# A convolution-attention model in one kernel: pieces of side work kept off the first two turns of a segment, and their ScalarE operations issued a turn later

## The chip, the cores and the metric

The kernel runs on one core of one Trainium2 chip. The metric is the time of the launch on the device, in microseconds, as the median of three runs. One further execution was taken with the hardware profiler; all durations below come from it.

## The reference, cut to what matters

The input is an image batch of four, 64 x 64 pixels with 128 channels, in fp32. Two layers follow each other.

```python
# layer 0, for each of the 4 images, N = 4096 pixels
c1 = conv3x3(elu(x), W1) + b1                    # 128 -> 128
a, b = split(conv3x3(c1, W2) + b2)               # 128 -> 2 x 128
c3 = a * sigmoid(b)
q, k, v = c3 @ Wq + bq, c3 @ Wk + bk, c3 @ Wv + bv   # 4, 4, 16 wide
atten = softmax(q @ k.T / 4, strictly causal) @ v
x = x + c3 + tile(atten, 8) @ W3 + b3
# layer 1, t = x as 4096 tokens
y = layernorm(t)
h = y + attention(y, 16 heads of 8, full) @ wo
t = t + h + (silu(h @ w1) * (h @ w3)) @ w2
y2 = layernorm(t)
t = t + mixture_of_8_experts(y2, top 2)
```

By far the largest part is the full attention of layer 1: 16 heads over 4096 queries and 4096 keys, for four images. Each score has to go through an exponential.

## The kernel before

**Steps.** The attention of layer 1 is cut into steps. A step (`attention_step`, L774) takes four heads (a group g), 512 queries (a block c) and 128 keys (kt): its part `scores` issues four matmuls into two PSUM tiles `s` of 128 x 1024 (there are three such buffers) and two exponentials on ScalarE into tiles `e`; its part `values` issues the matmuls of e with the values `vg` that add up in the PSUM tile `acc`. There is one `acc`, one bank. The causal attention of layer 0 has steps of its own (`first_step`, L699), 36 for each image. In all there are 4096 + 144 = 4240 steps, hence 8480 exponentials.

**Segments.** All steps of one g and c, or a part of their keys, are a segment. `plan` (L1101) lists 152 segments in a fixed order: for image 0 first segments over a quarter of the keys (8 of 8 steps), then over half of them (16 segments of 8 or 16 steps), then over the rest (32 of 16 or 32 steps); 32 of 32 steps for each later image. `stream()` (L1118) walks over the plan and gives out one step after the other; if a segment's operands are not there yet it gives None. It issues, on SP's queue, the loads of queries (`qx`), values (`vg`) and keys (`f_kx` from `d_k`) ahead of their use. After a segment's last values VectorE copies `acc` to a tile `at` (or adds it to an earlier part). Where the segment ends the keys, `by_token` is put into the list `urgent` and runs one turn after the next; otherwise `at` is stored to DRAM.

**Turns.** The main loop (L1184) runs once per turn: it issues the scores of one step, inserts at most one piece of other work, and then issues values. `finish(2)` holds the values of two steps back: in a turn, the values are those of the step of two turns ago. All engines work in the order written (`InOrder`), each instruction as soon as what it waits for is there.

**Pieces.** All other work is written as generators. A `yield us, kind` ends a piece and gives its TensorE time; `fillers` is the list of generators and works from its front. `convolutions` (L392), `first_attention` (L525) and `second_operands` (L604) prepare an image, under one filler of 149 us; `last_part` (L833, 20.8 us) finishes 512 tokens of an image. A piece that ends with "held" is the first half of one that shares the PSUM bank `m`. The turn's budget, `credit`, grows by `rate`; `rate` is 1 while image 0 is prepared and later the work left in `fillers` over the steps left to 40 before the image's end. A piece is inserted when the credit is positive, or when the stream waits, or when something urgent may run.

**Inside the pieces.** `winograd` (L341) computes a 3 x 3 convolution of 16 image rows in four column terms q with two pairs of products each; `final` makes the output of q = 2 and q = 3. For the gate half of the second convolution `final` adds on VectorE and issues a tanh on ScalarE; the rest (`gates`) is kept in the list `late` until the next pair. `elu` (in `convolutions`) treats chunks of 512 pixels in a pipeline of three stages: c_ (transposes on TensorE and evictions), b_ (the sum `pos`), a_ (the minimum `neg` and its exp). `last_part` has a tanh after each of three products and an exp of the router.

Before the main loop `run_alone` prepares the first two blocks of image 0 with no steps beside; after it the last part of the last block runs alone.

Of the kernel before, what the change touches and what calls it, by code (L numbers as in the profile page):

```python
# [115 lines left out]
def fast_path(ctx: ExitStack, tc: tile.TileContext, a: dict, where: dict, out: bass.AP, verdict):  # L116
# [33 lines left out]
    def chunk(tag, name=None):  # L150
        return wk.tile([P, QB], FP, tag=tag, bufs=CHUNKS.get(tag, 1), name=name or tag)
# [10 lines left out]
    def bank():  # L162
        return s_tile()[:, :QB] if alone[0] else m_tile()
# [177 lines left out]
    def winograd(u, cols, v, bias, used, final):  # L341

        late = []
        for q, j in enumerate(COLS):
            sd = chunk("sd")
            s, d = wk.tile([P, QB // 2], FP, tag="sums", bufs=1, name="sums"), sd[:, : QB // 2]
            for pair in ((1, 2), (0, 3)):
                ps = bank()
                part = [ps[:, : QB // 2], ps[:, QB // 2 :]]
                for m, i in zip(part, pair):  # L350
                    product(m, u[:, 4 * i + j, cols], v[q][:, i])
                    if i == pair[0]:
                        yield 0.46, "held"
                if pair[0] == 1:
                    if alone[0]:
                        act.activation(sd, ps, AF.Copy)
                    else:
                        dve.tensor_copy(sd, ps)
                    dve.tensor_tensor(s, d, sd[:, QB // 2 :], ALU.add)
                    dve.tensor_tensor(d, d, sd[:, QB // 2 :], ALU.subtract)  # L360
                    while late:
                        late.pop(0)()
                else:
                    t = chunk("neg", "t2")
                    if q == 0:

                        dve.scalar_tensor_tensor(t[:, : QB // 2], part[0], bias, s, ALU.add, ALU.add)
                        dve.scalar_tensor_tensor(t[:, QB // 2 :], d, bias, part[1], ALU.add, ALU.subtract)
                    else:
                        dve.tensor_tensor(t[:, : QB // 2], part[0], s, ALU.add)  # L370
                        dve.tensor_tensor(t[:, QB // 2 :], d, part[1], ALU.subtract)
                    used(q)
                    if q == 0:
                        one = t
                    elif q == 1:
                        both, less = chunk("pos", "both"), chunk("pos", "less")
                        (dve if alone[0] else pool).tensor_tensor(both, one, t, ALU.add)
                        pool.tensor_tensor(less, one, t, ALU.subtract)
                    elif q == 2:
                        late.append(final(0, t, both, ALU.add))  # L380
                    else:
                        late.append(final(1, less, t, ALU.subtract))
                yield 0.46, "stop"
        if late[0] is not None:
            yield 0.0, "stop"
            late.pop(0)()

# [4 lines left out]
    def convolutions(b, st):  # L392
# [4 lines left out]
        def elu(n):  # L397

            todo = range(made[0], n)
            made[0] = max(made[0], n)  # L400
            neg, pos = {}, {}
            for at in range(len(todo) + 2 if todo else 0):
                a_, b_, c_ = (todo[i] if 0 <= i < len(todo) else None for i in (at, at - 1, at - 2))
                if c_ is not None:
                    r, k = divmod(c_, 2)
                    ps = bank()
                    transposed(pos[c_], ps)
                    put = [(r, slice(1 + 8 * k, 9 + 8 * k), slice(0, 8))]
                    if k == 0 and r > 0:
                        put.append((r - 1, slice(17, 18), slice(0, 1)))  # L410
                    if k == 1 and r < 3:
                        put.append((r + 1, slice(0, 1), slice(7, 8)))
                    for band, to, of in put:
                        dve.tensor_scalar(
                            e_band[band % 2][:, to, 1 : IMG + 1], rows(ps)[:, of], -1.0, None, ALU.add
                        )
                if b_ is not None:

                    pos[b_] = chunk("pos")
                    dve.scalar_tensor_tensor(pos[b_], xs[b_], 0.0, neg[b_], ALU.max, ALU.add)  # L420
                    if b_ + 2 < NQ:
                        xs.append(load_x(b, b_ + 2, "xe"))
                if a_ is not None:
                    neg[a_] = chunk("neg")
                    dve.tensor_scalar(neg[a_], xs[a_], 0.0, None, ALU.min)
                    act.activation(neg[a_], neg[a_], AF.Exp)
                yield (0.0 if c_ is None else 0.6), "stop"

        def first(r):
            band = c_band[r % 2]  # L430
            inner = tiles(band[:, 1:17, 1 : IMG + 1])

            def final(h, x, y, op):
                x, y = (ap.rearrange("p (i y x) -> p i y x", i=2, y=8) for ap in (x, y))
                dve.tensor_tensor(inner[:, :, :, :, h], x, y, op)
                return lambda: None

            return final

        def second(r, gate):  # L440
            c3 = st.c3
            whole = tiles(c3.rearrange("p (y x) -> p y x", x=IMG))

            def final(h, x, y, op):
                shape = "p (i y x) -> p i y x"
                to = whole[:, :, :, :, h]
                if not gate:
                    x, y = (ap.rearrange(shape, i=2, y=8) for ap in (x, y))
                    dve.tensor_tensor(to, x, y, op)
                    return lambda: None  # L450

                g = x if h == 0 else y
                dve.tensor_tensor(g, x, y, op)
                act.activation(g, g, AF.Tanh, scale=0.5)
                g = g.rearrange(shape, i=2, y=8)

                def gates():
                    for i in range(2):
                        dve.scalar_tensor_tensor(to[:, i], g[:, i], 1.0, to[:, i], ALU.add, ALU.mult)

                return gates

            return final

# [368 lines left out]
    def last_part(b, c):  # L833
# [25 lines left out]
        for n, (lo, size) in enumerate(FCH):  # L859
            ps = bank()  # L860
            yield from halves(ps, fw1[:, lo : lo + size], hT, size)
            h1, th = chunk("neg", "h1"), chunk("sd", "th")
            dve.tensor_copy(h1[:size], ps[:size])
            act.activation(th[:size], h1[:size], AF.Tanh, scale=0.5)
            yield 0.46, "stop"
            ps = bank()
            yield from halves(ps, fw3[:, lo : lo + size], hT, size)
            dve.scalar_tensor_tensor(h1[:size], ps[:size], 0.5, h1[:size], ALU.mult, ALU.mult)
            dve.scalar_tensor_tensor(gT[n][:size], th[:size], 1.0, h1[:size], ALU.add, ALU.mult)
            yield 0.46, "stop"  # L870
# [52 lines left out]
        dve.tensor_reduce(m0, lg, AX.X, ALU.max)  # L923
        dve.tensor_tensor(lg, lg, over(m0), ALU.subtract)
        pr = small("pr", [4, NE])
        act.activation(pr, lg, AF.Exp)
        yield 0.95, "stop"
        yield 0.0, "stop"
        m1, w1 = top(pr, "a")
        rest = small("rest", [4, NE])  # L930
# [182 lines left out]
                        plan.append(Segment(b, run, g, c, 0, 4 * n, n, base))  # L1113
            had = n
    steps_left = [sum(s.hi - s.lo for s in plan if s.b == b) for b in range(B)]
    now = [0]

    def stream():  # L1118
        in_kx, vg_of = [None] * 4, {}
# [15 lines left out]
        for at, seg in enumerate(plan):  # L1135
# [12 lines left out]
            follower = plan[at + 1] if at + 1 < len(plan) else None  # L1148
            for kt in range(seg.lo, seg.hi):
                steps_left[seg.b] -= 1  # L1150
                if seg.lo > 0 and kt == seg.lo + 4:

                    part.append(chunk("part"))
                    sp.dma_start(out=part[0], in_=scratch[seg.b]["p"][seg.g, seg.c])
                yield attention_step(seg.b, seg, kt, 8 * seg.place(kt // 8) + kt % 8, qx, vg, part)
                if follower and follower not in ahead and follower.ready():
                    bring(follower)
                if kt % 8 == 7:

                    for later in plan[at + 1 :]:  # L1160
                        quarters = [q for q in range(later.lo // 8, later.hi // 8) if later.place(q) == seg.place(kt // 8)]
                        if quarters:
                            if later.ready():
                                key_quarter(later, quarters[0])
                            break
# [18 lines left out]
    while True:  # L1184
# [19 lines left out]
            within = steps_left[b] - 40 if b + 1 < B else min(steps_left[b] - 40, 160)  # L1204
            rate = sum(us for _, us in fillers) / max(1, within)
        credit = min(0.7, credit + rate)
        if waiting or credit > 0.0 or urgent and not held[0]:
            credit -= insert()
        finish(2)
    finish(0)  # L1210
# [724 lines left out]
```

## Time and profile before

| | |
|---|---|
| runs | 8383.02, 8379.8, 8378.74 us; median 8379.8 us |
| profiled execution | 8383.2 us; its span, first to last instruction, 8381.4 us |
| granted TensorE clock, mean | 0.981 |
| ScalarE (ACT) busy | 7919.2 us, of it 7836.1 us in 8480 exponentials |
| TensorE (PE) busy | 8082.3 us |
| VectorE (DVE) busy | 2543.8 us |
| GpSimd (POOL) busy | 711.6 us |
| TensorE waiting for the copy of acc (`at`) | 60.4 us in 53 waits |
| ScalarE waiting for scores (`s`) | 180.7 us in 164 waits |
| ScalarE waiting for VectorE's `t` (gate) and `neg` (elu) | 33.6 and 43.3 us |

In the lines of a profile a group is named by its output and inputs, as `e<-s`, with its shapes and count; after the bar stands its busy time and the mean of one in ns, and after the second bar the time that the engine stood idle just before such instructions, with what ended it. In an order of time each line has its start, its length and, in brackets, the idle time before it with its releaser. `PE m` is the bank of pieces, `PE s` the scores. Matmuls are pipelined, so a busy TensorE need not be at its peak. Most instructions carry one line number, that of the helper which issues them, so they are told apart by tile names.

### The profile page before, as it was taken

What the parts mean: (1) busy time and instruction counts of PE and PEld (TensorE: products, weight loads), DVE (VectorE), ACT (ScalarE), POOL (GpSimd) and SP (SyncE); (2) the same over time, 40 slices, a digit from 0 to 9 for tenths busy, and PEclk for the clock granted to TensorE, in tenths of its full rate; (3) what the DMA queues carried; (4) which work ended last, traced back from release to release, by engine and by line L of the source; (5) the groups of instructions that cost most, each with busy time, mean ns of one, the idle gap of its engine ahead of it and who ended that gap; (6) DMA issues with size and microseconds to landing.
All of it is one profiled execution on the core that took longest, in us unless ns stands there. A gap on an engine that the chain in (4) does not pass through costs nothing. (4 is left out here: it accounts for less than half of the span.)

```text
span 8381.4 us, 173763 instructions
## 1 busy us (share of the span) xinstructions
PE 8082.3 (96%) x73785; PEld 2565.1 (31%) x73785; DVE 2543.8 (30%) x5279; ACT 7919.2 (94%) x8698; POOL 711.6 (8%) x597
## 2 busy tenths in 40 slices
PE   4899999999999999999999999999999999999998
PEld 3222222223333332333333233233333333332333
DVE  7433122223322223333332222333333332221123
ACT  1899999999999999999999999999999999999996
POOL 5101101000000003110000000311100000000000
PEclk7999999999999999999999999999999999999998
DMA  1221010101100001101110000001101111011110
GB/s 54 76 66 66 19 38 23 40 23 48 44 17 19 22 11 31 33 29 46 34 30 11 26 15 17 28 30 44 33 33 43 37 37 43 31 38 34 54 53 32
DMA packets 239541, 295.99 MB, mean 35 GB/s; under 512 B 81731, under 2 KB 153891, under 8 KB 238755
## 3 DMA queue, kind: packets, MB, share of 16 engines
q1 hardware_dynamic: 234739, 283.03, 10.6%
q8 instruction: 580, 9.50, 0.5%
q10 hardware_dynamic: 4016, 1.77, 0.1%
q14 instruction: 206, 1.69, 0.1%
HBM read 185.12 MB, written 99.61 MB: 34 GB/s over the span
## 5 line engine op out<-in xcount | busy, mean ns | idle before, releaser
L105 ACT ACTIVATE e<-s 128x1024 f32<-128x1024 f32 x8480 | 7836.1, 1083 | 191.0 <-PE s L105 180.7
L105 PE MATMUL acc<-e,vg 128*9 128x512 f32 x32768 | 4362.5, 598 | 61.2 <-DVE at L105 60.4
L105 PE MATMUL s<-qx,f_kx 32*128 32x512 f32 (+1 forms) x16960 | 2795.9, 497 | 68.3 <-ACT e L105 51.4
L105 PEld LDWEIGHTS s<-qx,f_kx 32*128 32x128 f32 (+1 forms) x16960 | 1121.4, 182 | 4074.7 <-ACT e L105 3821.9
L105 PEld LDWEIGHTS acc<-e,vg 128*9 128x9 f32 x32768 | 707.3, 90 | 861.3 <-issue 448.5
L105 PE MATMUL m<-v,f_wino 128*32 128x256 f32 x5360 | 435.1, 397 | 9.6 <-DVE t L105 7.1
L105 DVE TENSOR_TENSOR by_e<-m,gate 128x512 f32<-128x512 f32 x248 | 171.5, 691 | 869.3 <-PE m L105 869.3
L105 POOL TENSOR_TENSOR v<-r 128x1024 f32<-128x1024 f32 x128 | 249.4, 1954 | 1277.4 <-PE m L105 1258.1
L105 DVE COPY sd<-m 128x512 f32<-128x512 f32 x167 | 115.5, 691 | 726.0 <-PE m L105 726.0
L105 PE MATMUL m<-f_we,y2T 128*32 128x256 f32 x3968 | 318.4, 393 | 0.5 <-DVE nt L105 0.5
L105 POOL TENSOR_TENSOR rs<-ve,f_minus_half 128x4 f32<-128x4 f32 x64 | 65.2, 1019 | 2972.5 <-DVE ve L105 2819.6
L105 DVE TENSOR_REDUCE added<-by_e 128x128 f32<-128x1024 f32 x128 | 255.2, 1994 | 4.4
L105 POOL TENSOR_TENSOR t<-t,h 128x512 f32<-128x512 f32 x32 | 40.9, 1278 | 2456.3 <-DVE h L105 2456.3
L105 PE MATMUL m<-hT,f_fw 128*32 128x256 f32 (+1 forms) x2728 | 236.1, 391 | 0.0
L105 DVE TENSOR_TENSOR t<-m,sums 128x256 f32<-128x256 f32 x126 | 53.5, 425 | 465.5 <-PE m L105 465.5
L105 DVE SCALAR_TENSOR_TENSOR h<-m,h 128x512 f32<-128x512 f32 (+1 forms) x93 | 64.2, 690 | 411.3 <-PE m L105 411.3
L105 DVE TENSOR_TENSOR t<-m,t 128x512 f32<-128x512 f32 x62 | 42.9, 692 | 446.3 <-PE m L105 446.3
L105 DVE COPY h<-m 128x512 f32<-128x512 f32 (+1 forms) x93 | 64.2, 690 | 357.0 <-PE m L105 357.0
L105 PEld LDWEIGHTS m<-v,f_wino 128*32 128x32 f32 x5360 | 107.1, 108 | 177.2 <-issue 152.5
L105 DVE COPY at<-acc 128x512 f32<-128x512 f32 x130 | 89.6, 689 | 233.2 <-PE acc L105 232.7
L105 PE MATMUL m<-e,f_v 128*32 128x512 f32 (+2 forms) x1128 | 149.7, 574 | 0.0
L105 DVE TENSOR_TENSOR e<-e,f_consts 128x128 f32<-128x128 f32 x128 | 30.2, 295 | 346.9 <-ACT e L105 346.9
(259 smaller groups left out, 3751.3 us busy)
## 6 DMA issues: line engine op xcount, KB each, us to landing
f_kx<-d_k SPq DMA_DIRECT2D x139, 512.0 KB, 4.1
qx<-d_q SPq DMA_DIRECT2D x152, 256.0 KB, 2.7
d_q<-two SPq DMA_DIRECT2D x64, 512.0 KB, 3.6
vg<-d_v SPq DMA_DIRECT2D x32, 576.0 KB, 4.2
d_k<-two SPq DMA_DIRECT2D x32, 512.0 KB, 3.3
d_v<-vc SPq DMA_DIRECT2D x32, 288.0 KB, 3.1
xe<-in_x_dram SPq DMA_DIRECT2D x32, 256.0 KB, 2.9
xt<-in_x_dram SPq DMA_DIRECT2D x32, 256.0 KB, 3.8
```

Of the source, the lines that this page charges most:

```text
L105: made = op(*args, **kw)
```

## The change

In the first two turns of a segment no piece is inserted unless the stream waits or something urgent may run; the first segment and those whose operands were not brought ahead are excepted (`quiet`). In `winograd` the tanh of the gate is no longer issued with its addition but at the start of the next pair, the entries of `late` are taken one at each pair's start, and what is left is given out with an empty piece each; layers without a gate leave nothing in `late`. In `elu` the stages b_ and a_ come ahead of c_. In `last_part` the tanh and the router's exp are issued at the start of the following piece.

```diff
@@ winograd
             for pair in ((1, 2), (0, 3)):
+                if late:
+                    late.pop(0)()
                 ps = bank()
...
-                    while late:
-                        late.pop(0)()
...
-                        late.append(final(0, t, both, ALU.add))
+                        late += final(0, t, both, ALU.add)
                     else:
-                        late.append(final(1, less, t, ALU.subtract))
+                        late += final(1, less, t, ALU.subtract)
                 yield 0.46, "stop"
-        if late[0] is not None:
+        while late:
             yield 0.0, "stop"
             late.pop(0)()
@@ elu
+                if b_ is not None:
+                    pos[b_] = chunk("pos")
+                    dve.scalar_tensor_tensor(pos[b_], xs[b_], 0.0, neg[b_], ALU.max, ALU.add)
+                    if b_ + 2 < NQ:
+                        xs.append(load_x(b, b_ + 2, "xe"))
+                if a_ is not None:
+                    neg[a_] = chunk("neg")
+                    dve.tensor_scalar(neg[a_], xs[a_], 0.0, None, ALU.min)
+                    act.activation(neg[a_], neg[a_], AF.Exp)
                 if c_ is not None:
...
-                if b_ is not None:
...
-                if a_ is not None:
...
@@ first(r) and second(r, gate), final
-                return lambda: None
+                return []
...
-                act.activation(g, g, AF.Tanh, scale=0.5)
-                g = g.rearrange(shape, i=2, y=8)
+                by_y = g.rearrange(shape, i=2, y=8)
+
+                def tanh():
+                    act.activation(g, g, AF.Tanh, scale=0.5)
 
                 def gates():
                     for i in range(2):
-                        dve.scalar_tensor_tensor(to[:, i], g[:, i], 1.0, to[:, i], ALU.add, ALU.mult)
-
-                return gates
+                        dve.scalar_tensor_tensor(to[:, i], by_y[:, i], 1.0, to[:, i], ALU.add, ALU.mult)
+
+                return [tanh, lambda: None, gates]
@@ last_part
             dve.tensor_copy(h1[:size], ps[:size])
+            yield 0.46, "stop"
             act.activation(th[:size], h1[:size], AF.Tanh, scale=0.5)
-            yield 0.46, "stop"
...
         pr = small("pr", [4, NE])
+        yield 0.95, "stop"
         act.activation(pr, lg, AF.Exp)
-        yield 0.95, "stop"
+        yield 0.0, "stop"
         yield 0.0, "stop"
@@ stream and the main loop
-    now = [0]
+    now, quiet = [0], [False]
...
                 steps_left[seg.b] -= 1
+
+                quiet[0] = kt < seg.lo + 2 and at > 0 and not late
...
-        if waiting or credit > 0.0 or urgent and not held[0]:
+        if waiting or credit > 0.0 and not quiet[0] or urgent and not held[0]:
             credit -= insert()
```

## The prediction

> **What bounds the kernel now.** I read the page first, then ScalarE's waits past the start-up (600 to 8315 us), then the order of time around single waits. On the page:
>
> ```profile
> PE 8082.3 (96%) x73785; PEld 2565.1 (31%) x73785; DVE 2543.8 (30%) x5279; ACT 7919.2 (94%) x8698; POOL 711.6 (8%) x597
> L105 ACT ACTIVATE e<-s 128x1024 f32<-128x1024 f32 x8480 | 7836.1, 1083 | 191.0 <-PE s L105 180.7
> ```
>
> Two engines look full, but only one is. ScalarE does 8480 exponentials in 7836.1 us, 0.924 us each, so a turn (two of them) costs 1.85 us. For TensorE I took starts of the scores from the order of time: 5000.47, 5002.34, 5003.74. A turn with a piece takes 1.87 us, a turn without one 1.40. About two turns in three hold a matmul piece after batch 0, so TensorE's mean is near 1.7 us: it runs ahead of ScalarE by the three score buffers and waits for them (its weight loads wait 3822.7 us for e). **ScalarE sets the pace; what counts is where it stands idle.** The whole idle time is 8381.4 - 7919.2 = 462 us. Its waits from 600 to 8315:
>
> ```profile
> ACT e L105 <- PE s L105: 117.4, 138, 5.2
> ACT t L105 <- DVE t L105: 20.1, 22, 1.5
> ACT neg L105 <- DVE neg L105: 7.3, 6, 2.9
> ACT e L105 <- ACT e L105: 1.9, 9, 0.3
> ```
>
> The columns are the total, the number and the longest. So 147 us lie in the long middle; the other 315 are start-up, the two changes of batch 0's key range, and the tail. Why scores come late is seen at 4340 us, the last turns of a segment's results:
>
> ```profile
> 4341.75 1.94 DVE L105 TENSOR_REDUCE added<-by_e 128x128 f32<-128x1024 f32 x1
> ...
> 4343.93 0.68 DVE L105 COPY at<-acc 128x512 f32<-128x512 f32 x1
> 4344.67 0.12 PEld L105 LDWEIGHTS acc<-e,vg 128*9 128x9 f32 x8 [2.33 <-DVE at L105]
> 4344.67 1.04 PE L105 MATMUL acc<-e,vg 128*9 128x512 f32 x8 [1.85 <-DVE at L105]
> ...
> 4346.24 4.69 ACT L105 ACTIVATE e<-s 128x1024 f32<-128x1024 f32 x5 [1.96 <-PE s L105]
> ```
>
> The copy of acc stands in VectorE's queue behind a piece's sum of 1.94 us. TensorE may not overwrite acc, waits 1.85 us, and the next scores stand behind those values: ScalarE is idle 1.96 us. The second kind is direct:
>
> ```profile
> 5903.68 1.67 DVE L105 TENSOR_TENSOR t<-t,both 128x512 f32<-128x512 f32 x1
> ...
> 5905.72 0.63 ACT L105 ACTIVATE t<-t 128x512 f32<-128x512 f32 x1 [1.49 <-DVE t L105]
> 5906.25 7.41 ACT L105 ACTIVATE e<-s 128x1024 f32<-128x1024 f32 x8
> ```
>
> The tanh waits for VectorE though two exponentials of the next turn could run; the line below shows that they start only after it.
>
> **The Trainium skill.** "TensorE: Matmul & The Clock Gate", Part 1, says that TensorE falls to half clock after an idle window of about 3.4 us and needs a busy one to return. The trace agrees: after the 4.43 us wait at 8007 the eight values take 1.90 us, not 1.04, and a second ScalarE wait of 1.45 us follows. "ScalarE: Activation LUTs", Table sets, puts exp and tanh in one set, so a moved tanh costs no table load; the trace has one load in all. "Perfetto Trace Analysis", Per-engine timelines, has each ScalarE instruction wait in a queue ahead of the engine; the 1.49 us above shows that queue blocking.
>
> **The change part by part.**
>
> (1) Quiet turns. The values of a step trail it by two turns, so the last values of a segment are issued at the end of its follower's second turn and the copy right behind them; the follower's first values come a turn later. VectorE's work ahead of the copy is that of pieces in turns 1 and 2: just the turns that become empty. In the listing of VectorE, 38 of the 133 copies past 700 us begin without idle time before them, that is, behind a piece. I went through ScalarE's 41 waits of 0.8 us or more past 700 us (83.1 us) and looked for a wait of acc for at within 6 us before each: 18 places, with their repeats at half clock 57.1 us; two more at 497 and 543 add 3.6. Of these 60.7 I take **50**. The rest may stay: a layernorm piece (at 8002 it keeps VectorE until 8006.5) issued in the turn just before the segment still reaches the copy. Bounds 35 and 61.
>
> (2) Tanh later. Direct waits 20.1 us, and 4.6 more from 260 to 435; five waits of 1.3 us follow such a tanh by 4 to 8 us (at 1146, 1528, 3665, 3859, 5733: 6.6 us). Of these 31 I take **29**: the tanh now comes after another pair of exponentials, 1.85 us, against waits of at most 1.49. The gates come two pieces later and no engine but VectorE needs them soon. Bounds 20 and 31. The 96 tanh and 32 exp of the last part, moved likewise, had no wait outside the tail, as VectorE was done early: 0. In the tail ScalarE waits for VectorE either way. Were the cover gone (VectorE a turn behind), each could wait up to 1.5 us as the tanh above; being issued a turn later makes that less likely, not more.
>
> (3) The elu order. Exp waits for two VectorE operations (0.69 and 0.42 us) and no more for the eviction behind TensorE's transposes. Of 7.3 us I take **6** (4 to 7). The load of xe keeps its place in SP's queue.
>
> (4) Lost turns. While batch 0 is prepared the credit is full and every turn takes one piece, so a quiet turn delays preparation by a turn. The first stage has 8 segments of 8 turns; 7 of them lose 2: 14 turns. That stage already ends too early (busy time of each engine in the stretch, then ScalarE's order of time):
>
> ```profile
> core 0: us, PE busy (x) PEld busy (x) DVE busy (x) ACT busy (x) POOL busy (x), PEclk, DMA share, GB/s
> 360.00:378.00 18.00, 9.60 (x114) 3.44 (x106) 10.32 (x16) 0.86 (x1) 0.00 (x0) 0.69 0.62 208
> ```
>
> ```profile
> 377.14 5.65 ACT L105 ACTIVATE e<-s 128x1024 f32<-128x1024 f32 x6 [17.83 <-PE s L105]
> ```
>
> ScalarE, busy 0.86 of 18 us, stands 17.83 us until the second key range is stored (d_k issued at 368.31) and loaded. The 14 pieces move into this bare gap. There, from 358.4 to 368.3, some six pieces took 10 us; but first-attention steps moved with them bring ScalarE's own work along. At about 1 us each I add **13** (0 to 25). The second stage: preparation ends at 718.51 (the last d_k), its last segment's eighth turn, where keys for the third range are fetched, is at 793: 39 turns of slack. It loses 15 x 2 quiet turns and some 4 for more yields, 34: free, by 5 turns. If that cover goes, a late load as above, some 10 us.
>
> From batch 1 on the rate is worked out anew each turn from what is left, pieces use about 0.8 of the turns (with empty ones), and quiet takes 64 of 1024: 0.94 are left, so 0. The extra yields (net 4 a batch, and one in each last part) are turns without matmul. A crowded turn after the quiet ones costs TensorE 1.87 against 1.85: hidden by the lead that the two empty turns of 1.40 give.
>
> DMAs: pieces moved two turns bring their stores and loads behind the follower's qx and vg in SP's queue; these are issued in turn 1 and used a segment later. In batch 0 the order of d_k and f_kx may shift single waits (one of 6.6 us stands at 488): plus or minus 7. The start-up reorders elu and tanh too, with ScalarE idle for DVE t and neg there: plus or minus 5, taken as 0, since a longer chain is at its place.
>
> **Sum**: -50 - 29 - 6 + 13 = -72 us. The profiled execution took 8383.2 us around a span of 8381.4, 3.4 above the median of 8379.8, so it is a usual one; 8383.2 - 72 = 8311 for it, and 8379.8 - 72 = **8308** for the median.
>
> **Rivals.** (A) The forecast, 0.68. (B) The wait moves on: VectorE's backlog comes from the turn before the segment or the crowded third turn, so that of the 60.7 us only 20 go, and tanh gives 20. For it: layernorms and sums of 2 to 6 us; 0.38 us waits for at with no backlog. Against: in the cases read, the late operation belonged to a matmul of turn 2. Time: 8380 - 20 - 20 - 5 + 13 = 8348. 0.20. (C) Slower: batch 0 starves. If the second stage's slack of 39 turns is less than what quiet turns and yields take, preparation ends after the stage; then both gaps are bare: 14 + 34 pieces at 2.2 us (two chained matmul halves, eviction and a wait) = 106, less 85 of gains: 8401. It decides from 39 lost turns on; I count 34. 0.06. (D) The flag hardly acts: it is skipped where a piece is urgent, and stays as it was during first-attention steps. But an urgent piece is born only at the end of turn 2, and such steps start after a turn with a piece, where the flag is off. Then only tanh and elu would count, some -35, or -15 if the pieces then crowd: 8345 to 8365. 0.06.
>
> **Numbers.** Best case: 61 + 31 + 7 and some 15 of the 35.6 us of short waits (104 under 0.8 us) gained, nothing lost: 8266. The low side of A and B is 8379.8 - 35 - 20 - 4 + 35 = 8356. Range 8266 to 8356; that leaves out C and some of D. A measurement of this kernel tells about 0.2% (17 us) from no change: faster 0.88, same 0.06, slower 0.06.
>
> **What would show it.** Right: PE's wait of acc for at falls from 60.4 to below 25; ACT's wait for t to under 3 and for neg in the middle to about 1; the idle time before e from 600 to 8315 from 117 to 60-75; the gap at 377 grows to about 30 us; busy times of ScalarE stay at 7919. Wrong: acc's wait stays over 40 (B or D), a new gap near 800 us (C), or ScalarE's idle falls while TensorE's busy share in the middle reaches 99% with the turn no shorter.

## The result and the profile after

The changed kernel takes **8297.96 us** (median of four runs, 8293.22 to 8302.43) against 8381.41 us (8378.74 to 8385.31) of the kernel before beside it: a ratio of 0.990, 95% interval 0.9883 to 0.9917. That is 83.4 us less; the forecast was 72 less. The profiled execution took 8302.43 us around a span of 8300.7 us, so it is the longest of the four.

The page of the changed kernel, its busy times and two groups (after the second bar: the idle time just before such instructions):

```profile
PE 8073.1 (97%) x73713; PEld 2576.8 (31%) x73713; DVE 2557.3 (31%) x5278; ACT 7915.4 (95%) x8699; POOL 708.5 (9%) x597
...
L105 ACT ACTIVATE e<-s 128x1024 f32<-128x1024 f32 x8480 | 7842.5, 1087 | 133.4 <-PE s L105 124.3
L105 PE MATMUL acc<-e,vg 128*9 128x512 f32 x32768 | 4337.9, 595 | 1.7 <-DVE at L105 1.7
```

ScalarE has the same work, 7915.4 us against 7919.2; its idle time fell from 462.2 to 385.3 us, and these two differences (76.9 + 3.8) are the 80.7 us between the spans. TensorE's wait for the copy of `acc` is nearly gone: 1.7 us, where the same line of the kernel before has 60.4:

```profile
L105 PE MATMUL acc<-e,vg 128*9 128x512 f32 x32768 | 4362.5, 598 | 61.2 <-DVE at L105 60.4
```

ScalarE's waits in the long middle, 600 to 8235 us (total, number, longest; the middle ends 80 us earlier than before's):

```profile
ACT e L105 <- PE s L105: 53.8, 88, 3.1
ACT neg L105 <- DVE neg L105: 7.4, 4, 3.3
ACT e L105 <- ACT e L105: 1.5, 8, 0.2
```

Scores now cost it 53.8 us instead of 117.4, the tanh (`t`) nothing instead of 20.1, the elu's exp (`neg`) 7.4 as before. From 600 us to the last exponential (which ends at 8310.84 us before, at 8223.18 after) ScalarE's whole idle time fell from 154.5 to 68.7 us, by 85.8, and waits with a name make up 84 of it. Both ends lost a little. The tail behind the last exponential took 77.5 us instead of 70.5, and by 600 us ScalarE had done 358.75 us of work, against 360.76.

The end of a segment, in order of time in the changed kernel:

```profile
4354.65 10.22 ACT L105 ACTIVATE e<-s 128x1024 f32<-128x1024 f32 x11
...
4358.01 1.05 PE L105 MATMUL acc<-e,vg 128*9 128x512 f32 x8
...
4359.12 0.69 DVE L105 COPY at<-acc 128x512 f32<-128x512 f32 x1 [9.06 <-PE acc L105]
4359.87 1.05 PE L105 MATMUL acc<-e,vg 128*9 128x512 f32 x8
```

The copy finds VectorE idle for 9.06 us, starts as soon as the last values are there, and the follower's first values come 0.06 us after it ends (4359.12 + 0.69 = 4359.81) with no wait in brackets. ScalarE's line, from 4354.65 for 10.22 us, runs through without a break. And the tanh:

```profile
5885.05 1.67 DVE L105 TENSOR_TENSOR t<-t,both 128x512 f32<-128x512 f32 x1
...
5890.96 0.68 ACT L105 ACTIVATE t<-t 128x512 f32<-128x512 f32 x1
5891.48 5.66 ACT L105 ACTIVATE e<-s 128x1024 f32<-128x1024 f32 x6
```

It runs 4.2 us after its addition ends (5890.96 - 5886.72), so its input has long been there.

What it paid: the gap before image 0's second key range, ScalarE's order of time.

```profile
387.10 5.65 ACT L105 ACTIVATE e<-s 128x1024 f32<-128x1024 f32 x6 [36.91 <-PE s L105]
```

The 17.83 us have become 36.91.

### The profile page after: what moved, and what is told of

It is laid out like the page before. It is cut to its first block, busy times and chain, and to the rows that moved or that the text cites. A ratio compares the mean times of both kernels' runs of the same rounds, so it can differ in the third digit from the quotient of the medians.

```text
span 8300.7 us, 173662 instructions
## 1 busy us (share of the span) xinstructions
PE 8073.1 (97%) x73713; PEld 2576.8 (31%) x73713; DVE 2557.3 (31%) x5278; ACT 7915.4 (95%) x8699; POOL 708.5 (9%) x597
## 4 chain that ended last, share of the span: by engine, by line
PE 87%; issue 7%; DVE 3%; ACT 1%; POOL 1%; DMA 1%; SPq 0%; ACTq 0%; POOLq 0%; DVEq 0%
PE acc L105 41%; PE s L105 28%; PE m L105 18%; ACT e L105 1%; DVE h L105 1%; DVE added L105 0%; DMA nt<-d_a 0%; DVE t L105 0%; POOL v L105 0%; DMA f_kx<-d_k 0%; POOL rs L105 0%; DVE two L105 0%; DMA xe<-in_x_dram 0%; DVE at L105 0%; DVE by_e L105 0%
```

## The experiments

Each was timed in five rounds beside the kernel before. Ratios are to that kernel, with the 95% interval. "Changed kernel" means the kernel after.

**1. Quiet turns alone**, all else as before.

```diff
-        if waiting or credit > 0.0 or urgent and not held[0]:
+        if waiting or credit > 0.0 and not quiet[0] or urgent and not held[0]:
```

> Only the quiet turns are added to the kernel before; the order of ScalarE's operations and of elu stays. Theory (the parts add up): TensorE's wait of acc for at falls from 60 to about 2 us as in the changed kernel, the gap before the second key range grows from 18 to about 37 us, ScalarE's direct waits for the gate's t stay near 20 us past 600 us: 8381 - 57 + 15 = about 8340. Rival (the two parts overlap: without the later tanh the crowded turns after the quiet ones lose again what was won): 8360 or more. Rival (quiet is all that counts): 8300.

Measured 8328.05 us, 0.9934 (0.9921 to 0.9948), -53.9 us. ScalarE's waits past 600 us:

```profile
ACT e L105 <- PE s L105: 59.5, 104, 2.8
...
ACT t L105 <- DVE t L105: 20.1, 22, 1.2
```

Past 600 us TensorE's wait for `at` fell from 54.8 to 1.1 us, and the waits for scores by 57.9 us, while the tanh waits stayed at 20.1 us to the tenth. So the quiet turns act on the first kind of wait only, and on nearly all of it. The gap was 34.78 us long.

**2. Later ScalarE operations alone**: the changed `winograd`, `final` and `last_part`, without the quiet turns and the elu order.

> Only the later ScalarE operations (the gate's tanh, the last part's tanh and exp) are added to the kernel before; elu and the inserting of pieces stay. Theory: the waits for t past 600 us go from 20 to about 0, acc's wait for at stays at 55 to 60, the gap before the second key range stays near 18: 8381 - 29 = about 8352. Rival (the tanh was covered by ScalarE's own queue, the gain was in the quiet turns): 8375 to 8385.

Measured 8318.70 us, 0.9924 (0.991 to 0.9937), -63.2 us: twice what was expected. The tanh wait was gone as expected, but waits for scores fell too, from 117.4 to 82.3 us, and TensorE's wait for `at` in the middle was down by more than a quarter, from 54.8 us:

```profile
PE acc L105 <- DVE at L105: 39.4, 36, 6.5
```

Nothing in the moved tanh explains this directly. It does bring more empty pieces with it (the entries of `late`), and these shift every later piece against the ends of segments. Run 5 tests that.

**3. The elu order alone.**

> Only the order of elu's three stages is changed in the kernel before. The prediction gave it 6 us. Theory now, from the changed kernel's order of time: the min waits for the load of xe, which waits for the sum before it; with the stages nearer together this load is less covered, so the waits for neg past 600 us stay at 6 to 10 us and the time within 5 us of 8381. Rival (the eviction ahead was the cause, the rest came from elsewhere): neg below 2 us and 8375 or less.

Measured 8388.97 us, 1.0011 (1.0004 to 1.0017), +7.1 us: a small loss. Its waits from 600 to 8235 us:

```profile
ACT e L105 <- PE s L105: 120.8, 125, 5.2
ACT t L105 <- DVE t L105: 20.2, 22, 1.5
ACT neg L105 <- DVE neg L105: 10.0, 6, 2.9
```

Again six waits of the elu's exp, with the same longest of 2.9 us; their total rose from 7.3 to 10.0. The reorder doesn't remove what that exp waits for, which is of two kinds. In the kernel before three of the six (4.8 us) are for an image's first load of `xe`. In the changed kernel, VectorE's and ScalarE's order of time at such a place:

```profile
788.40 0.43 DVE L105 TENSOR_SCALAR neg<-xe 128x512 f32<-128x512 f32 x1 [5.80 <-DMA xe<-in_x_dram]
...
788.86 0.63 ACT L105 ACTIVATE neg<-neg 128x512 f32<-128x512 f32 x1 [3.34 <-DVE neg L105]
```

The minimum waits for a load that was issued at 783.03, one piece earlier. The median load of `xe` takes 2.9 us from issue to landing, more than a turn of 1.85. At an image's first chunk there is no eviction yet that could stand ahead of the minimum.

Two more (2.1 us) are behind VectorE operations that run beside GpSimd's `v` (terms of the next convolution). The first of these places in run 3:

```profile
3168.73 8.00 POOL L105 TENSOR_TENSOR v<-r 128x1024 f32<-128x1024 f32 x4
...
3172.47 2.47 DVE L105 SCALAR_TENSOR_TENSOR pos<-xe,neg 128x512 f32<-128x512 f32 x1 [6.08 <-ACT neg L105]
...
3174.87 2.14 DVE L105 TENSOR_SCALAR neg<-xe 128x512 f32<-128x512 f32 x1
...
3175.00 1.11 PE L105 MATMUL m<-f_consts,pos 128*128 128x128 f32 x4 [1.08 <-DVE pos L105]
...
3177.04 0.63 ACT L105 ACTIVATE neg<-neg 128x512 f32<-128x512 f32 x1 [2.77 <-DVE neg L105]
```

The sum took 2.47 us and the minimum 2.14, against medians of 0.69 and 0.43; the exp waited for the minimum and TensorE's transposes for the sum. At the two places of this kind the exp waited 2.77 and 2.73 us, in the kernel before 0.99 and 1.07. Right behind them ScalarE waited for scores 4.2 us (1.80, 0.71 and 1.73), before 0.6. Together that is 7.1 us more, about as much as run 3 lost. Only one wait of the kernel before, 0.4 us, stood behind an eviction. The order alone doesn't settle whether sum and minimum meet `v`: run 11 below, in the old order, has waits of 1.07 and 2.71 us there.

**4. Quiet turns only once image 0 is prepared.**

```diff
-                quiet[0] = kt < seg.lo + 2 and at > 0 and not late
+                quiet[0] = kt < seg.lo + 2 and at > 0 and not late and batches[0].second == NQ
```

> The changed kernel with quiet turns only once image 0 is prepared. Theory (lost turns lengthen the gap before the second key range): the gap falls from 37 back to about 18 us, some waits of acc for at return before 720 us (8 waits, about 8 us, of which ScalarE feels 5): 8298 - 19 + 5 = about 8284. Rival (the longer gap is ScalarE work that only changed its place, so nothing is lost by it): 8298 or up to 8305.

Measured 8295.75 us, 0.9895 (0.988 to 0.9911): 2.2 us below the changed kernel, where 14 had been expected. The gap did shrink to 14.43 us. The core's busy times from 0 to 600 us, first the changed kernel, then this one (the fourth pair of numbers is ScalarE):

```profile
core 0: us, PE busy (x) PEld busy (x) DVE busy (x) ACT busy (x) POOL busy (x), PEclk, DMA share, GB/s
0.00:600.00 600.00, 464.15 (x3602) 185.15 (x3602) 308.77 (x589) 358.75 (x405) 165.15 (x150) 0.87 0.20 65
```

```profile
core 0: us, PE busy (x) PEld busy (x) DVE busy (x) ACT busy (x) POOL busy (x), PEclk, DMA share, GB/s
0.00:600.00 600.00, 467.02 (x3798) 188.46 (x3798) 321.47 (x615) 367.82 (x412) 168.94 (x153) 0.88 0.21 66
```

22.5 us less gap gave 9.1 us more of ScalarE's work by 600 us, since gaps of 7.03 us at 356 and 5.29 us at 488 came in; and the middle's idle time, up to the last exponential, was 73.8 us, 5.1 more, about as much as the elu's exp waited more (12.2 against 7.4 us). The two kernels' runs overlap, so the 2.2 us are no measurable gain. The length of one gap is a poor price for lost preparation: work that doesn't stand in it comes out elsewhere.

**5. The empty pieces without the later tanh**: run 2, with the tanh and the exp issued where they were before.

```diff
-                def tanh():
-                    act.activation(g, g, AF.Tanh, scale=0.5)
+                act.activation(g, g, AF.Tanh, scale=0.5)
...
-                return [tanh, lambda: None, gates]
+                return [lambda: None, lambda: None, gates]
```

> The kernel before with only the number of pieces changed as in the later-ScalarE kernel: the same empty pieces are added and dropped, and the gates come as late, but every tanh and exp is issued at its old place; no quiet turns, old elu. It shows what the shift of all pieces against the segments' ends does by itself. Theory (of the 63 us that the later-ScalarE kernel won, some 30 are tanh waits and the rest is that other pieces now fall on the segments' ends): waits for t stay near 20 us past 600 us, acc's wait for at falls from 55 to about 40, time 8381 - 63 + 30 = about 8348. Rival (all 63 us come from the later tanh, by stalls of TensorE that follow a tanh): acc's wait near 55, time 8375 to 8385.

Measured 8350.99 us, 0.9964 (0.995 to 0.9977), -31.0 us.

```profile
ACT e L105 <- PE s L105: 90.4, 121, 7.0
...
ACT t L105 <- DVE t L105: 20.0, 22, 1.2
```

So half of run 2's gain comes without any tanh moved: scores wait 27.0 us less (117.4 - 90.4), though the profiled run was the slowest of the five (8360.01 us). The later tanh itself is the rest, 8350.99 - 8318.70 = **32.3 us**. This kernel moves pieces only by what a few more empty ones take; where they then stand against the ends of 152 segments is chance. It gives out the gates later, too, as run 2 does; but of the 47 waits for `at` past 600 us in the kernel before only one, 0.9 of 54.8 us, had a gate right ahead of the copy, so that can explain little.

**6 and 7. One quiet turn each**: only the second (`kt == seg.lo + 1`), and only the first (`kt == seg.lo`), in the changed kernel.

> The changed kernel with only a segment's second turn empty; pieces go into the first again. Theory (VectorE has the whole second turn of 1.4 to 1.9 us to finish a piece of the first; only long ones, layernorms and sums of 2.9 to 6 us, still reach the copy): acc's wait for at past 600 us rises from 1 to 5 to 12 us, the gap before the second key range falls from 37 to about 28 us: 8298 plus or minus 6. Rival (the first turn's pieces matter as much): acc's wait 25 or more, 8320.

> The changed kernel with only a segment's first turn empty; pieces go into the second again. Theory (the second turn's pieces stand right ahead of the copy): acc's wait for at is near that without quiet turns, 35 to 55 us, time 8298 + 20 to 8298 + 40, less 8 us of the shorter gap: 8310 to 8330. Rival (the first turn is the one that counts): 8300 or less and acc's wait under 15 us.

Only the second: 8286.49 us, 0.9888 (0.9873 to 0.9903), 11.5 us *below* the changed kernel and below what was expected, though TensorE's wait for `at` came back in part (7.7 us); the gap was 29.78 us instead of 36.91. The runs do not overlap (8283.56 to 8289.22 against 8293.22 to 8302.43), though the intervals of the ratios overlap. Only the first: 8347.55 us, 0.9961 (0.9947 to 0.9975), slower than the 8310 to 8330 expected, and 29 us slower than run 2, which has no quiet turn at all (nor the new elu order, which alone cost 7). TensorE's wait, then the order of time at one place, both with only the first turn quiet:

```profile
PE acc L105 <- DVE at L105: 54.6, 49, 4.4
```

```profile
7442.49 1.11 DVE L105 TENSOR_SCALAR y<-t,mv,rs 128x128 f32<-128x128 f32 x4 [1.20 <-POOL rs L105]
7443.52 0.68 DVE L105 COPY at<-acc 128x512 f32<-128x512 f32 x1
...
7444.26 1.79 PE L105 MATMUL acc<-e,vg 128*9 128x512 f32 x8 [4.42 <-DVE at L105]
...
7446.88 1.94 ACT L105 ACTIVATE e<-s 128x1024 f32<-128x1024 f32 x2 [4.89 <-PE s L105]
```

A layernorm stands right ahead of the copy, with GpSimd's step (1.20 us) inside it. A piece held back in turn 1 is inserted in turn 2, straight ahead of the copy. The turn that does most of the work is the second. The first buys a little and costs more. In the profiled runs (18.9 us apart in span) ScalarE's idle time from 600 us to the last exponential was 74.9 us with the second turn alone, 6.2 more than with both. But it had done 371.08 us of work by 600 us instead of 358.75, and the tail took 71.1 us instead of 77.5. So the first turn's price lies in the preparation of image 0 and in the tail, not in the long middle.

**8. A layernorm with one more empty turn behind it** (`second_operands`), in the changed kernel. What was left in the middle included three waits of about 3 us in which TensorE waits for the layernorm. One of them in the changed kernel, in order of time:

```profile
3542.30 4.83 DVE L105 TENSOR_SCALAR h<-xt,mv,rs 128x128 f32<-128x128 f32 x4 [1.13 <-POOL rs L105]
3542.32 4.73 POOL L105 TENSOR_TENSOR r<-f_c_band 128x528 f32<-128x528 f32 x4
...
3547.19 0.33 PE L105 MATMUL m<-f_consts,h 128*128 128x128 f32 x1 [0.94 <-DVE h L105]
...
3549.91 1.94 ACT L105 ACTIVATE e<-s 128x1024 f32<-128x1024 f32 x2 [2.78 <-PE s L105]
```

```diff
         layernorm(t, h)
-        for _ in range(2):
+        for _ in range(3):
             yield 0.0, "stop"
```

> The changed kernel with one more empty piece between a layernorm of the second operands and the transposes of its result. Theory (of the waits that are left, those near 1349, 3549 and 5595 us are TensorE waiting for h, whose four scalings take 4.8 us beside GpSimd's row terms): TensorE's wait of m for h past 600 us falls from 9.5 to about 2 us and the time by 8 to 14: about 8287. Rival (the stall of h is hidden by the score buffers in most cases, or the added turns only move other pieces): 8293 to 8303.

Measured 8292.08 us, 0.9894 (0.9878 to 0.9909), 5.9 us below the changed kernel, about half of what was expected. TensorE's waits for `h` past 600 us, 9.5 us in the changed kernel, were gone. ScalarE's waits in the middle:

```profile
ACT e L105 <- PE s L105: 33.2, 77, 2.6
ACT neg L105 <- DVE neg L105: 16.5, 5, 6.5
```

The wait for scores fell by 20.6 us, but the elu's exp took 9.1 of it back: pieces had shifted again, and image 1's first load of `xe`, which landed 7.6 us after its issue, alone held it for 6.5 us. The runs of the two kernels do not quite touch (8290.67 to 8292.87 against 8293.22 to 8302.43), but the intervals of their ratios overlap: of the net only the sign is likely, and the waits tell the mechanism.

**9. Joined**: only the second turn quiet and only once image 0 is prepared (runs 4 and 6), with the extra turn of run 8.

> The changed kernel with three edits together: only a segment's second turn is empty, and only once image 0 is prepared; and one more empty piece after the second operands' layernorm. Theory (the three effects stand in different places): the gap before the second key range back to about 15 to 18 us, acc's wait for at past 600 us 5 to 12 us, TensorE's wait of m for h below 2 us: 8286 - 6 - 8 = about 8272. Rival (the gap's length is made up by later waits, as quiet turns off during preparation alone brought only 2 us): 8280 to 8286.

Measured 8272.30 us, 0.987 (0.9853 to 0.9886), as expected: 25.7 us below the changed kernel. The gap was 12.55 us, scores kept ScalarE waiting for 40.6 us in the middle, and the elu's exp for 11.7.

**10. Joined, with an empty turn after each elu piece**, so that a load of `xe` has two turns.

```diff
                 yield (0.0 if c_ is None else 0.6), "stop"
+                if not alone[0]:
+                    yield 0.0, "stop"
```

> The joined kernel with one empty piece after each of elu's pieces beside steps. Theory (what keeps neg late is the load of xe, issued one turn before the min that needs it; two turns of 1.85 us cover it): ScalarE's waits for neg past 600 us fall from some 10 to 16 us to below 4, and the time by 6 to 12 us against the joined kernel: about 8264. Rival (neg waits for VectorE's queue, not for the load): neg stays at 8 or more and the time within 4 us of the joined kernel.

Measured 8260.85 us, 0.9858 (0.9842 to 0.9875), 11.5 us below run 9. ScalarE's waits in the middle:

```profile
ACT e L105 <- PE s L105: 34.3, 79, 1.6
...
ACT neg L105 <- DVE neg L105: 6.4, 3, 2.9
```

The waits of the exp fell from 11.7 to 6.4 us; 6.3 us more came from scores (40.6 to 34.3). It is not below 4 as expected: the three waits that stay (2.46, 1.05 and 2.89 us) are each for an image's first load, issued ahead of elu's first piece, where no empty piece was added. Of run 9's six, those that went are two beside GpSimd's `v` (2.75 and 2.60 us) and one of 0.2 us for a load. So the time fell as expected, but hardly for the reason that was expected.

**11 and 12. The old elu order** in runs 9 and 10.

> The joined kernel with elu's stages in the old order (eviction, sum, min). Theory (the new order is worth nothing or a little less than nothing, since the load of xe is what neg waits for; alone it cost 7 us): time 0 to 7 us below the joined kernel, neg's waits past 600 us 2 to 6 us lower. Rival (elu's new order helps once the rest is out of the way): 3 to 6 us above the joined kernel.

> The joined kernel with an empty piece after each of elu's pieces beside steps and with elu's stages in the old order. Theory (the order of elu matters only through the load of xe; once two turns cover it, either order gives the same): within 4 us of 8261. Rival (the old order has a worth of its own, 7 us as in the two pairs before): 8254 or less.

Run 11: 8265.08 us, 0.9862 (0.9846 to 0.9879), 7.2 us below run 9, the size that the order cost alone in run 3, though the waits for `neg` fell by 1.4 us only (11.7 to 10.3) and not by the 2 to 6 expected. Run 12: 8257.81 us, 0.9853 (0.9837 to 0.987), 3.0 us below run 10; their runs overlap, so here the order makes no difference that these runs tell. It is the fastest kernel of the series, 123 us below before and 40 us below the changed kernel.

## Why the prediction was right, by its steps

The forecast, that ScalarE sets the pace and its named waits shrink, holds: -83.4 against -72, in the range and on the right side, and the waits that it listed are those that moved. Its four terms, against what the runs showed:

| step | forecast | measured |
|---|---|---|
| (1) quiet turns and (4) lost turns together | -50 + 13 = -37 | -53.9 (run 1) |
| (2) tanh later | -29 | -32.3 (run 2 less run 5) |
| (3) elu order | -6 | +7.1 (run 3) |
| empty pieces shift the rest | 0 | -31.0 alone (run 5) |

The first three rows add up to -53.9 - 32.3 + 7.1 = -79.1, near the -83.4; so what is left for the shift next to the quiet turns is about 4 us, not 31, if the other rows add up (runs of one kernel spread over 5 to 14 us). The likely reason is that both remove the same waits, those for `at`, past 600 us: 54.8 us before, 42.2 with the shift alone, 1.1 with quiet turns alone. One wait can't be gained twice. The kernel with both and no later tanh was not run.

That the sum came so near is in part luck: the first row gained 17 us more than forecast, the third 13 us less.

**(1) right, and sized too low.** It kept 10.7 of 60.7 us back for pieces of the turn just before the segment that would still reach the copy. They did not: 1.1 us of waits for `at` stayed. In run 1 the waits for scores in the middle fell by 57.9 us. Its reading that the damage comes from pieces in turns 1 and 2 was half right. Runs 6 and 7 show that it is mostly turn 2: with only that one quiet, 7.7 us of waits for `at` stayed, with only the first, 54.6.

**(2) right,** in its place and within 3.3 us. What the tanh waited for was itself a delay: in the kernel before 18 of the 22 waits (19.2 of 20.1 us) followed an addition that took 1.67 to 1.75 us beside GpSimd's `v`, and 0.69 us elsewhere. Issued a turn later, the tanh no longer feels it. "The extra yields (net 4 a batch, and one in each last part) are turns without matmul", costed at 0, was wrong as a statement about the part alone: the place of every later piece changes, and run 5 shows 31 us for it. The forecast was safe from this error only because step (1) had already counted the waits concerned.

**(3) wrong in sign.** The step that failed: "Exp waits for two VectorE operations (0.69 and 0.42 us) and no more for the eviction behind TensorE's transposes." Of the six waits in the kernel before, 7.3 us, three (4.8 us) were for a load, two (2.1 us) for a minimum that took 2.15 us beside GpSimd and not 0.42, and one (0.4 us) stood behind the eviction: the new order had 0.4 us to win there, not 6. The trace of before could have told it: the longest wait for `neg`, 2.9 us, is more than two times the two VectorE operations together (1.11 us). Where the order lost 7 us is seen in run 3; that it was the order, and not chance, that put the sum and the minimum beside `v` is not shown.

**(4) right in its mechanism.** The gap grew by 19.1 us, not 13, within the 0 to 25. But the price of the stage as a whole is smaller: by 600 us ScalarE was only 2.0 us behind the kernel before, although run 4 shows that 9.1 us could be had there. The parts pull apart there: 368.50 us of ScalarE's work was done by then in run 2 and 355.70 in run 1. The second stage's cover held: preparation ended at 780.36 us instead of 718.51, and the keys of the third range were fetched at 793.05. The forecast's slack was 39 turns less 34; 12.7 us, some 7 turns, were left. One price it had at nothing: the tail took 7.0 us more. With the quiet turns alone (run 1) it took 72.8 us and with the later operations alone (run 2) 70.7, so neither part explains the 77.5 us; the cause stays open.

**The signs that it named.** Waits of `acc` below 25: 1.7. Waits of `t` under 3: none. The gap about 30: 36.91. ScalarE's busy time at 7919: 7915.4. The idle time before e in the middle 60 to 75: 53.8, lower. `neg` about 1: 7.4, the miss of step (3). TensorE's busy share in the middle did reach the 99% that was named as a sign of being wrong (98.4 before, 99.2 after); but that sign asked for a turn no shorter as well, and the kernel got 83.4 us faster. Rivals B and D needed waits for `at` to stay, C a gap near 800; neither is there.

## What to carry to other kernels

When work is slotted between the turns of a pacing engine, find which turn stands ahead of a single-buffered accumulator's eviction and keep that one free: here the second turn did most of it, and with the first free as well the kernel was 11.5 us slower. Issue an operation of the pacing engine a turn after what it reads. Before giving VectorE a new order, look at each wait that it should remove: of six here, three ended with a load and two with an operation that took 2.15 us instead of 0.42. An empty piece is not neutral where pieces meet the ends of segments by chance: compare with a kernel that has the same empty pieces and nothing else.

## What the runs showed of the hardware

**VectorE beside GpSimd.** The four scalings of a layernorm take 1.11 us when GpSimd is idle (`y`, 7442.49 in run 7) and 4.83 us beside four row operations of GpSimd that take 4.73 us (`h`, 3542.30 in the changed kernel). One kind of instruction is 4.4 times as long. The Trainium skill, "SBUF — State Buffer", Who interferes with whom, says that some VectorE instructions hold a port pair in turn with GpSimd, the other being blocked for the whole instruction. The trace fits: each of the four scalings lasted 1.15 to 1.43 us, about as long as one row operation. It fits at the gate's additions (or subtractions) in the kernel before, too:

```profile
5902.86 1.94 POOL L105 TENSOR_TENSOR v<-r 128x1024 f32<-128x1024 f32 x1 [5.06 <-PE m L105]
...
5903.68 1.67 DVE L105 TENSOR_TENSOR t<-t,both 128x512 f32<-128x512 f32 x1
```

The addition ends 0.55 us after `v` (5905.35 against 5904.80), as it does at all 18 places where a tanh waited 0.99 us or more past 600 us; eight additions without GpSimd beside them took 0.69 us. No run here takes GpSimd's work away to show that it is the cause.

**Half clock after short waits.** The Trainium skill, "TensorE: Matmul & The Clock Gate", Part 1, says that half clock follows an idle window of about 3.4 us. After the wait of 4.42 us in run 7 the eight values took 1.79 us instead of 1.04, which agrees. But shorter waits brought it too. Two stretches of the kernel before, one right behind the other (PEclk is the granted clock):

```profile
core 0: us, PE busy (x) PEld busy (x) DVE busy (x) ACT busy (x) POOL busy (x), PEclk, DMA share, GB/s
5760.07:5763.48 3.41, 1.41 (x14) 0.24 (x12) 2.26 (x5) 2.51 (x3) 0.81 (x1) 1.00 0.20 77
5763.48:5766.89 3.41, 3.41 (x16) 0.96 (x16) 0.55 (x2) 1.94 (x2) 0.00 (x0) 0.50 0.00 0
```

A wait of 2.00 us lies in the first, in which TensorE was still busy for 1.41 us; the second ran at half clock. Between 600 and 8200 us the trace has 34 such halvings, of 3.4 or 6.8 us, and in the 3.41 us ahead of each TensorE stood idle for 31 to 95% by its records. The length of a wait alone doesn't decide it: right behind two waits of 1.98 and 1.99 us values took 1.90 us, behind others of 1.98, 2.00 and 2.40 us still 1.05. In this case a window that was idle only in part was enough, and the measurement decides.
